# Attention beside key tiles: the other work in pieces of 128 tokens, and row sums inverted on VectorE

## The chip, the cores and the metric

The kernel runs on one core of a Trainium2 chip. The metric is the device time of one execution in microseconds; the median of three runs is shown, and one further execution was profiled. The engines are TensorE (PE in the profile, its weight loads PEld), VectorE (DVE), ScalarE (ACT), GpSimd (POOL) and SyncE (SP, which here only issues DMAs).

## What is computed

The input x has shape (4, 2048, 512). It is normalized over its last axis; the output is x plus attention plus a sparse expert layer, both of the normalized xn:

```python
qkv = xn @ w_qkv                     # 16 heads of 32
q, k = spectral_filter(q), spectral_filter(k)      # a fixed 32x32 map per head
attn = softmax(q @ k.T / sqrt(32)); a = (attn @ v) @ w_out + b_out
probs = softmax(xn @ w_gate)         # 8 experts, the best one, first 100 tokens of each
f = combine(dispatch(xn) @ w_expert + b_expert)
return x + a + f
```

All of it is in float32. The softmax needs a maximum and a sum of each row of 2048 scores; the row sums are inverted and multiplied onto the product with v before w_out.

## The kernel before

The spectral filter is folded into the weights at the start. Then the program goes through 16 head groups (k; 4 batches x 4 groups of 4 heads), in each through 4 query blocks of 512 tokens (n), and in each through 16 key tiles of 128 tokens (j). Two key tiles make a window (WIN, line 40). So there are 1024 tiles and 512 windows.

A tile's work (lines 918 to 938) is done for two pairs of heads, u = 0 and 1. TensorE writes minus the row maximum into two PSUM banks (`shift`, 3-row bf16 matmuls, negm in the profile), computes scores for a later block's maxima into two more (`max_matmuls`, k,q), and adds the scores (`scores`, q,k). ScalarE takes the exponential of each bank into an `even` or `odd` tile; VectorE reduces the maxima (`max_reduce`, part). Last come the products of the tile before with v (`products`), which VectorE adds to `num`. The eight banks are handed out in turn by `bank()`, whoever asks.

All other work is put behind the tiles as steps. The `agenda` holds a list for each window; a list's first half stands behind the even tile, the second behind the odd (lines 916, 917, 943). InOrder (line 71) keeps this order on every engine's queue, SP's included from line 786 on. What stands on the agenda:

- `projections(k + 1)`: twelve blocks of 512 tokens for the next group, 8 of `query_key` and 4 of `value`, placed at equal distances over the group. Each takes one bank and ends in one ScalarE copy. The weights wg have one buffer, so the load for group k + 2 follows the last block.
- `close_steps`, for each block that has ended: `fold` sums the exponentials over the partitions with TensorE and copies them (den). The four different rows travel to DRAM and back as a 128x16 tile (few), are inverted by VectorE, go to DRAM again and are spread over 32 partitions each (factor): seven DMAs on SP's queue. `divide` multiplies num by factor on GpSimd (ot). `result` projects 128 tokens with w_out (wo,ot) and copies them; `add` adds them to the output by an accumulating DMA.
- For a new batch: loading, `measure` (bn_stats on VectorE), `scale` (a power on GpSimd), `normalize` (ScalarE), `turn` (TensorE transposes of two token tiles, each copied by ScalarE), and the `route` of the expert layer, a chain of small steps and 16 scattering DMAs. The batch's groups 2 and 3 (k = 2, 3, 6, 7, 10, 11) carry this. From k = 12 on the expert layer itself is on the agenda.

At the start of each window stand the split of new maxima, an accumulating DMA (`pair`: even += odd of the window before) and GpSimd's running sums of the exponentials (`add_to`, two operations of 128x1024). With these GpSimd and the DMA engines have work in every window.

Of the kernel before, what the change touches and what calls it, by code (L numbers as in the profile page):

```python
# [38 lines left out]
SCALE = 1.0 / math.sqrt(DH)  # L39
WIN = 2  # L40
# [61 lines left out]
def attention_and_top1_experts(ctx: ExitStack, tc: tile.TileContext, a: dict, out: bass.AP):  # L102
# [118 lines left out]
    def token_stage(b):  # L221
# [38 lines left out]
        def turn(i):  # L260

            for j in (i, i + 1):
                px = bank()
                xn = held[j // TQ][:, j % TQ, :]
                for r in range(NR):
                    on.tensor.transpose(px[:, r * P : (r + 1) * P], xn[:, r * P : (r + 1) * P], ident)
                on.scalar.copy(xnT[:, :, j * P : (j + 1) * P], px.rearrange("p (r n) -> p r n", r=NR))
# [52 lines left out]
        def below_top():  # L320
            on.vector.reduce_max(top, logits, axis=AX.X)
            on.gpsimd.tensor_tensor(probs, logits, wide(top), ALU.subtract)
            on.scalar.activation(probs, probs, AF.Exp)
# [63 lines left out]
        route = [score, by_token, below_top, divide, best, ranked, first_best, place, carry_on, locate, note]  # L387
# [22 lines left out]
    def query_key(k, n, s):  # L410
        cols = slice(n * QB, (n + 1) * QB)
        pq = bank()
        for r in range(NR):
            columns(pq, wg[k][:, r, s, :], xnT[:, r, cols], start=(r == 0), stop=(r == NR - 1))
        if s == 0:
            qs[k, n] = qkv.tile([P, QB], F32, tag="q", name="q", bufs=5)
            on.scalar.copy(qs[k, n], pq)
        else:
            if n == 0:
                ks[k] = qkv.tile([P, S], F32, tag="k", name="k")  # L420
            on.scalar.copy(ks[k][:, cols], pq)

    def value(k, n):
        if n == 0:
            vs[k] = qkv.tile([P, NT, P], F32, tag="v", name="v")
        pv = bank()
        for t in range(TQ):
            i = n * TQ + t
            tok = slice(t * P, (t + 1) * P)
            for r in range(NR):  # L430
                columns(
                    pv[:, tok],
                    xnT[:, r, i * P : (i + 1) * P],
                    wg[k][:, r, 2, :],
                    start=(r == 0),
                    stop=(r == NR - 1),
                )
        on.scalar.copy(vs[k][:, n * TQ : (n + 1) * TQ, :], pv.rearrange("p (t d) -> p t d", t=TQ))

    def projections(k):  # L440

        order = [(query_key, 0, 1), (query_key, 0, 0)]
        order += [(query_key, n, 1) for n in range(1, NQ)] + [(query_key, 1, 0)]
        order += [(value, n) for n in range(NQ)] + [(query_key, n, 0) for n in range(2, NQ)]
        return [lambda f=f, at=at: f(k, *at) for f, *at in order]
# [203 lines left out]
    def close_steps(k, n, num, acc):  # L649
# [4 lines left out]
        def fold():  # L654
            den = work.tile([P, QB], F32, tag="den", name="den", bufs=1)
            on.scalar.copy(den, row_sums([acc]))
            held["sums"] = scratch.tile([HG, QB], F32, name="sums")
            on.sync.dma_start(out=held["sums"], in_=den[0::DH, :])

        def fold_here():  # L660

            held["factor"] = work.tile([P, QB], F32, tag="factor", name="factor", bufs=1)
            on.vector.reciprocal(held["factor"], row_sums([acc]))


        def fetch():
            held["few"] = small.tile([P, HG * QB // P], F32, name="few", bufs=2)
            on.sync.dma_start(out=held["few"], in_=held["sums"].rearrange("h (c e) -> (h c) e", e=HG * QB // P))

        def invert():  # L670
            on.vector.reciprocal(held["few"], held["few"])
            held["inverse"] = scratch.tile([HG, QB], F32, name="inverse")
            on.sync.dma_start(
                out=held["inverse"].rearrange("h (c e) -> (h c) e", e=HG * QB // P), in_=held["few"]
            )

        def spread():
            held["factor"] = work.tile([P, QB], F32, tag="factor", name="factor", bufs=1)
            for h in range(HG):
                on.sync.dma_start(  # L680
                    out=held["factor"][DH * h : DH * (h + 1)], in_=held["inverse"][h].partition_broadcast(DH)
                )

        def divide():
            held["ot"] = work.tile([P, QB], F32, tag="ot", name="ot", bufs=1)
            on.gpsimd.tensor_tensor(held["ot"], num, held["factor"], ALU.mult)
# [9 lines left out]
        if (k, n) == (B * NG - 1, NQ - 2):  # L696
            return [(3, fold_here), (4, divide), (5, result, 0), (5, result, 1), (6, result, 2), (6, result, 3), (7, add)]
        steps = [(2, fold), (3, fetch), (4, invert), (5, spread), (7, divide)]
        return steps + [(8, result, 0), (8, result, 1), (9, result, 2), (9, result, 3), (10, add)]
# [38 lines left out]
    first_projections = projections(0)  # L738
    scale(0, TQ, on.vector)
    for i in range(TQ):  # L740
        normalize(i)
        measure(TQ + i)
        if i % 2 == 1:
            turn(i - 1)
# [34 lines left out]
    ahead = {1: lambda: turn(4), 3: lambda: turn(6), 6: first_projections[2]}  # L779
    ahead.update({9: lambda: turn(8), 11: lambda: turn(10), 14: first_projections[3]})  # L780
    ahead.update({17: lambda: turn(12), 19: lambda: turn(14), 22: first_projections[4]})
    ahead.update({28: first_projections[5], 33: first_projections[6]})
    ahead.update({4 + j: lambda j=j: normalize(12 + j) for j in range(0, 2)})
    ahead.update({7 + j: lambda j=j: normalize(14 + j) for j in range(0, 2)})
    first_projections = first_projections[7:]
# [20 lines left out]
    GW = NQ * NW  # L806
    agenda = [[] for _ in range(B * NG * GW + 2 * NW)]

    def at(window, step, *args):
        agenda[window].append(lambda: step(*args))  # L810
# [11 lines left out]

    def place_experts(start):
# [3 lines left out]
        first = start + 18  # L827
        at(first, begin)
        for i in range(ST):
            at(first + 1 + i, fetch, i)  # L830
            at(first + 3 + i, measure, i)
        at(first + 11, scale)
        for i in range(ST + 2):
            at(first + 12 + i, expert, i)
        for i in range(ST):
            free = start + GW + i * NW + 11
            for step in (gather_row, add_row, scatter_row):
                at(free, step, i)
                free += 1

    def plan(k):

        b, c = divmod(k, NG)
        start = k * GW
        if k == 0:
            for i, step in enumerate(first_projections):
                at(i, step)
            for i, step in enumerate(first_route):
                at(NW + i, step)
            for n in range(NQ):  # L850
                at(1 + 4 * n, load, n)
                for i in range(TQ):
                    at(3 + 4 * n + i // 2, first_bias, n * TQ + i)
                at(5 + 4 * n, first_sums, n)
        if k == (B - 1) * NG:
            place_experts(start)
        if k + 1 == B * NG:
            return
        at(start + GW // 2, load_out_weights, k + 1)
        if k + 2 < B * NG:  # L860
            at(start + GW - 2, load_qkv_weights, k + 2)
        if k == 0:
            at(len(first_projections), load_qkv_weights, 1)
        first, last = len(first_projections) + 2 if k == 0 else 0, GW - 1
        if c == NG - 2 and b + 1 < B:

            at(start + 10, begin_stage, b + 1)
            for n, (come, go) in enumerate(((11, 19), (15, 23), (20, 28), (24, GW))):
                at(start + come, in_stage, 0, n)
                at(start + go, in_stage, 7, n)  # L870
            for i in range(NT):
                at(start + 13 + i + i // 8, in_stage, 1, i)
                at(start + 14 + i + i // 8, in_stage, 6, i)
            at(start + GW - 1, in_stage, 2)
            at(start + GW - 2, in_stage, 0, 0)
            at(start + GW + 1, in_stage, 0, 1)
        elif c == NG - 1:

            for n in (2, 3):
                at(start + 2 * n - 1, in_stage, 0, n)  # L880
            for i in range(NT):
                at(start + i // 2 + i // 8, in_stage, 3, i)
                if i % 2 == 1:
                    at(start + i // 2 + i // 8 + 1, in_stage, 4, i - 1)
            for i in range(len(first_route)):
                at(start + 10 + i, follow_route, i)
            first, last = 10, GW - 1
        steps = projections(k + 1)
        for i, step in enumerate(steps):
            at(start + first + (last - first) * i // len(steps), step)  # L890
# [12 lines left out]
    for k in range(B * NG):  # L903
        plan(k)
        for n in range(NQ):
            num = work.tile([P, QB], F32, tag="num", name="num")
            tiles = {}
            for w in range(NW):
                even, odd = w * WIN, w * WIN + 1
                if window in splits:  # L910
                    max_split(*splits.pop(window))
                if window in pairs:
# [3 lines left out]
                here = agenda[window]  # L916
                cut = (len(here) + 1) // 2
                for j in (even, odd):
# [24 lines left out]
                    for step in here[:cut] if j == even else here[cut:]:  # L943
# [12 lines left out]
            if not last:  # L956
                for after, *step in close_steps(k, n, num, tiles[NT - WIN]):
                    at(window + after, *step)
    products(*left)
    add_to(*adds.pop(window))  # L960
    for step in agenda[window]:
        step()
    close_last(k, n, num, [tiles[j] for j in (NT - 4, NT - 3, NT - 2, NT - 6, NT - 1)], y)
    for steps in agenda[window + 1 :]:
# [35 lines left out]
```

## Time and profile before

| | |
|---|---|
| median of 3 runs | 4454.81 us (4453.89 to 4457.47) |
| the profiled execution | 4463.09 us, its span 4461.3 us |
| mean granted TensorE clock | 0.993 |
| first key tile starts, last starts | 96.2 us, 4441.7 us |
| plain group 5 (1476.9 to 1738.5) | 261.6 us: PE 261.6, DVE 188.8, ACT 154.8, POOL 173.0 busy, DMA share 0.77 |
| group 2 (647.3 to 915.8) | 268.5 us: PE 266.3, DVE 200.3, POOL 190.3, DMA share 0.85 |
| group 3 (915.8 to 1212.1) | 296.3 us: PE 284.4, DVE 192.1, ACT 175.2, POOL 194.5, DMA share 0.73 |
| group 15 (4214.4 to 4441.7) | 227.3 us: PE 214.4, DVE 164.6, POOL 140.4, DMA share 0.87 |
| packets of the queue q1 (SP's DMAs) | 79,456, 93.89 MB, 7.0% of the DMA engines |

All instructions after the first few carry the line of one helper (L82), so they are told apart by their operands. A matmul in float32 leaves two records. The time of a matmul overlaps its neighbours', so the distance from one start to the next says more than the duration.

### The profile page before, as it was taken

What the parts mean: (1) busy time and instruction counts of PE and PEld (TensorE: products, weight loads), DVE (VectorE), ACT (ScalarE), POOL (GpSimd) and SP (SyncE); (2) the same over time, 40 slices, a digit from 0 to 9 for tenths busy, and PEclk for the clock granted to TensorE, in tenths of its full rate; (3) what the DMA queues carried; (4) which work ended last, traced back from release to release, by engine and by line L of the source; (5) the groups of instructions that cost most, each with busy time, mean ns of one, the idle gap of its engine ahead of it and who ended that gap; (6) DMA issues with size and microseconds to landing.
All of it is one profiled execution on the core that took longest, in us unless ns stands there. A gap on an engine that the chain in (4) does not pass through costs nothing. (4 is left out here: it accounts for less than half of the span.)

```text
span 4461.3 us, 106253 instructions
## 1 busy us (share of the span) xinstructions
PE 4369.7 (98%) x44398; PEld 1869.5 (42%) x44398; DVE 3130.6 (70%) x3634; ACT 2581.3 (58%) x4971; POOL 2958.8 (66%) x2009
## 2 busy tenths in 40 slices
PE   8999999999999999999999999999999999999998
PEld 4443443434434343443444434343443444434432
DVE  6667777766676777776667767777667676676776
ACT  3555565565555556556555555555655555555665
POOL 0677666775766766776677666767667674776773
PEclk9999999999999999999999999999999999999999
DMA  4677778886777777798677777888768876788788
GB/s 107 157 169 155 154 151 166 194 198 129 144 151 147 157 157 156 165 206 182 122 150 150 154 158 142 168 178 206 162 128 161 165 156 122 155 165 163 148 164 179
DMA packets 191546, 707.03 MB, mean 158 GB/s; under 512 B 47374, under 2 KB 52656, under 8 KB 125784
## 3 DMA queue, kind: packets, MB, share of 16 engines
q0 software_dynamic: 110432, 605.83, 69.6%
q1 hardware_dynamic: 79456, 93.89, 7.0%
q8 instruction: 347, 5.69, 0.5%
q14 instruction: 135, 1.11, 0.1%
q10 hardware_dynamic: 1176, 0.52, 0.0%
HBM read 76.03 MB, written 89.98 MB: 37 GB/s over the span
## 5 line engine op out<-in xcount | busy, mean ns | idle before, releaser
L82 DVE TENSOR_REDUCE part<-array 128x2 f32<-128x1024 f32 (+1 forms) x2313 | 2433.9, 1097 | 1218.5 <-PE array L82 1205.6
L82 POOL TENSOR_TENSOR even<-even 128x1024 f32<-128x1024 f32 x876 | 2133.1, 2550 | 215.1 <-DMA even<-odd 213.8
L82 PE MATMUL array<-k,q 32*128 32x512 f32 x8192 | 2221.7, 621 | 2.4 <-DVE part L82 1.7
L82 PE MATMUL array<-q,k 32*128 32x512 f32 x8192 | 2047.3, 593 | 1.3 <-issue 1.3
L82 ACT ACTIVATE even<-array 128x512 f32<-128x512 f32 x2048 | 1064.9, 601 | 453.0 <-PE array L82 443.1
L82 ACT ACTIVATE odd<-array 128x512 f32<-128x512 f32 x2048 | 1060.1, 602 | 434.7 <-issue 224.7
L82 POOL DMA_DIRECT2D even<-odd x510 | 460.1, 902 | 1101.7 <-ACT odd L82 887.8
L82 PEld LDWEIGHTS array<-k,q 32*128 32x128 f32 x8192 | 806.3, 183 | 167.7 <-DVE num L82 71.3
L82 PE MATMUL array<-negm,ones_b 3*128 3x512 bf16 x4096 | 792.4, 382 | 15.6 <-issue 5.2
L82 PEld LDWEIGHTS array<-q,k 32*128 32x128 f32 x8192 | 746.0, 185 | 13.2 <-issue 4.3
L82 DVE TENSOR_TENSOR num<-num,array 128x512 f32<-128x512 f32 x960 | 650.8, 678 | 34.4 <-PE array L82 19.3
L82 PEld LDWEIGHTS <-ones_b 3*128 3x128 bf16 x4096 | 202.1, 92 | 904.3 <-issue 776.6
L82 PE MATMUL array<-even,v 128*32 128x512 f32 x4096 | 548.8, 606 | 8.2 <-ACT odd L82 8.1
L82 PE MATMUL array<-odd,v 128*32 128x512 f32 x4096 | 548.4, 606 | 4.6 <-ACT even L82 4.5
L82 PE MATMUL array<-xnT,wg 128*32 128x512 f32 x4096 | 465.3, 595 | 1.8 <-DMA wg<-wd 1.1
L82 PE MATMUL array<-wo,ot 128*32 128x512 f32 x2048 | 264.4, 607 | 37.5 <-POOL ot L82 37.4
L82 PEld LDWEIGHTS array<-xnT,wg 128*32 128x32 f32 x4096 | 132.3, 110 | 307.9 <-issue 270.9
L82 PEld LDWEIGHTS array<-even,v 128*32 128x32 f32 x4096 | 81.0, 108 | 401.2 <-ACT odd L82 390.1
L82 ACT COPY y<-array 128x512 f32<-128x512 f32 x252 | 147.6, 586 | 173.8 <-PE array L82 173.0
L82 PEld LDWEIGHTS array<-odd,v 128*32 128x32 f32 x4096 | 81.1, 108 | 396.0 <-ACT even L82 388.0
L82 PEld LDWEIGHTS array<-wg,xnT 128*32 128x32 f32 x8192 | 227.0, 110 | 43.8 <-issue 26.2
L82 PE MATMUL array<-wg,xnT 128*32 128x128 f32 x8192 | 238.3, 273 | 2.7 <-issue 2.4
(127 smaller groups left out, 1370.6 us busy)
## 6 DMA issues: line engine op xcount, KB each, us to landing
even<-odd POOLq DMA_DIRECT2D x510, 1024.0 KB
out_dram<-y POOLq DMA_DIRECT2D x63, 1024.0 KB
xs<-in_L_attn_x_dram SPq DMA_DIRECT2D x30, 1024.0 KB
out_dram<-xs SPq DMA_DIRECT2D x16, 1024.0 KB
factor<-inverse SPq DMA_DIRECT2D x248, 64.0 KB
wg<-wd SPq DMA_DIRECT2D x15, 768.0 KB
wo<-in_L_attn_w_out_dram SPq DMA_DIRECT2D x16, 256.0 KB
negm<-row SPq DMA_DIRECT2D x192, 4.0 KB
```

The lines of the kernel that those rows point to most:

```text
L82: done = act(*args, **kwargs)
```

## The change

The agenda now has a list for each tile ("half") instead of each window, and a list of costs beside it. `query_key`, `value` and `turn` work on 128 tokens: a block becomes four pieces, each with its own bank and its own ScalarE copy; a query/key matmul has 128 columns and not 512. `spread` places a group's pieces in order, up to four tiles before the group's end, so that the sum of costs stays level; a piece, a result, a fold and a turn cost 1, a closing's inversion 0. The projections of the first group that run before the first tile remain whole.

`close_steps` copies the whole den, and eight `invert` steps of 64 columns, one behind each of eight tiles, invert it on VectorE; the seven DMAs and the scratch tensors are gone. `divide` moves from the agenda to `heads`, which stand at the start of a window, before pair and sums. Counted in tiles from the end of a block: fold 4 to 5, inversion 8 to 6-13, divide 14, results 16 to 19 become 15 to 18. For the last block but one of all: fold 7, two inversions behind each of tiles 8 to 11, divide 12, results 12 to 15. The route's exponential becomes a step of its own. The scale of a new batch moves from the last window of group 2 to four tiles before its end.

```diff
         def turn(i):
-            for j in (i, i + 1):
-                px = bank()
...
-                on.scalar.copy(xnT[:, :, j * P : (j + 1) * P], px.rearrange("p (r n) -> p r n", r=NR))
+            px = bank()
...
+            on.scalar.copy(xnT[:, :, i * P : (i + 1) * P], px.rearrange("p (r n) -> p r n", r=NR))
...
         def below_top():
             on.vector.reduce_max(top, logits, axis=AX.X)
             on.gpsimd.tensor_tensor(probs, logits, wide(top), ALU.subtract)
+
+        def exponentials():
             on.scalar.activation(probs, probs, AF.Exp)
...
-    def query_key(k, n, s):
-        cols = slice(n * QB, (n + 1) * QB)
-        pq = bank()
+    def query_key(k, n, s, first, last):
+        here, cols = slice(first * P, last * P), slice(n * QB + first * P, n * QB + last * P)
+        pq = bank()[:, here]
         for r in range(NR):
             columns(pq, wg[k][:, r, s, :], xnT[:, r, cols], start=(r == 0), stop=(r == NR - 1))
...
+            on.scalar.copy(qs[k, n][:, here], pq)
...
-    def projections(k):
+    def projections(k, tiles=1):
...
-        return [lambda f=f, at=at: f(k, *at) for f, *at in order]
+        return [
+            lambda f=f, at=at, t=t: f(k, *at, t, t + tiles) for f, *at in order for t in range(0, TQ, tiles)
+        ]
...
         def fold():
-            den = work.tile([P, QB], F32, tag="den", name="den", bufs=1)
-            on.scalar.copy(den, row_sums([acc]))
-            held["sums"] = scratch.tile([HG, QB], F32, name="sums")
-            on.sync.dma_start(out=held["sums"], in_=den[0::DH, :])
...
+            on.scalar.copy(held["den"], row_sums([ended[k, n][1]]))
...
-        def fetch():
...
-        def spread():
...
+        def invert(i):
+            at = slice(i * PART, (i + 1) * PART)
+            on.vector.reciprocal(held["factor"][:, at], held["den"][:, at])
...
-        steps = [(2, fold), (3, fetch), (4, invert), (5, spread), (7, divide)]
-        return steps + [(8, result, 0), (8, result, 1), (9, result, 2), (9, result, 3), (10, add)]
+            steps = [(7, 1, fold)] + [(8 + i // 2, 0, invert, i) for i in range(QB // PART)]
+            first = 12
+        else:
+            steps = [(5, 1, fold)] + [(6 + i, 0, invert, i) for i in range(QB // PART)]
+            first = 15
+        steps += [(first + t, 1, result, t) for t in range(TQ)]
+        return steps + [(first + TQ - 1 + first % 2, 0, add)], (first - first % 2, divide)
...
+    def spread(steps, last):
+        base = steps[0][1]
+        def places(level):
+            half, done, found = base, costs[base], []
+            for cost, first, _ in steps:
+                while half < first or done + cost / 2 > level * (half - base + 1):
+                    half += 1
+                    if half > last:
+                        return None
+                    done += costs[half]
+                done += cost
+                found.append(half)
+            return found
+        found = next(filter(None, (places(level / 32) for level in range(16, 400))))
...
-        steps = projections(k + 1)
-        for i, step in enumerate(steps):
-            at(start + first + (last - first) * i // len(steps), step)
+            done = spread([(1, ready if k == 0 else start, step) for step in pieces], last)
+        if k + 2 < B * NG:
+            at(done[-1] + 1, load_qkv_weights, k + 2)
...
                 if window in splits:
                     max_split(*splits.pop(window))
+                for step in heads[2 * window]:
+                    step()
                 if window in pairs:
                     pair(*pairs.pop(window))
...
-                    for step in here[:cut] if j == even else here[cut:]:
+                    for step in agenda[2 * window + (j == odd)]:
                         step()
```

## The prediction

> **What bounds the kernel now.** I read the page first, then the groups of instructions by form, TensorE's timeline tile by tile, the waits of TensorE, and last the busy times in stretches (one for each of the 16 head groups). From the page:
>
> ```profile
> span 4461.3 us, 106253 instructions
> PE 4369.7 (98%) x44398; PEld 1869.5 (42%) x44398; DVE 3130.6 (70%) x3634; ACT 2581.3 (58%) x4971; POOL 2958.8 (66%) x2009
> q8 instruction: 347, 5.69, 0.5%
> ```
>
> TensorE is the bound. What a key tile costs it is read from the timeline (start, duration, engine, operation, and in brackets the idle time before and its releaser), from the start of one tile's first shift matmul (negm) to the next tile's, and what a step behind a tile adds from the start of the products (even,v / odd,v) on:
>
> ```profile
> 1588.16 0.39 PE L82 MATMUL array<-negm,ones_b 3*128 3x512 bf16 x2
> ...
> 1590.30 1.07 PE L82 MATMUL array<-odd,v 128*32 128x512 f32 x8
> 1591.30 0.39 PE L82 MATMUL array<-negm,ones_b 3*128 3x512 bf16 x2
> ```
> ```profile
> 1580.59 1.06 PE L82 MATMUL array<-odd,v 128*32 128x512 f32 x8
> 1581.47 3.62 PE L82 MATMUL array<-xnT,wg 128*32 128x512 f32 x32
> 1585.02 0.39 PE L82 MATMUL array<-negm,ones_b 3*128 3x512 bf16 x2
> ```
> ```profile
> 1603.39 1.07 PE L82 MATMUL array<-odd,v 128*32 128x512 f32 x8
> 1604.28 3.68 PE L82 MATMUL array<-wg,xnT 128*32 128x128 f32 x128
> 1607.88 0.39 PE L82 MATMUL array<-negm,ones_b 3*128 3x512 bf16 x2
> ```
>
> A bare tile takes 3.14 us; products to next tile are 1.00 bare, 4.43 with a query/key block (+3.43), 4.49 with a value block (+3.49). One result adds 0.86, two 1.72: steps behind a tile add their pure time and no fixed cost. I compared all 1023 tile periods with 3.14 (2.20 at the end, where no maxima are left) plus such prices. What they take beyond that is 128 us in all; the rest is work. It is very uneven: groups 1, 5 and 9 have under 2 us each. So even placing has nothing to win in plain groups; it can only win back named stalls:
>
> ```profile
> PE array L82 <- POOL ot L82: 37.4, 15, 6.8
> PE array L82 <- issue: 9.9, 9, 2.8
> ```
> ```profile
> 807.21 0.39 PE L82 MATMUL array<-negm,ones_b 3*128 3x512 bf16 x2 [2.17 <-issue]
> 925.25 3.64 PE L82 MATMUL array<-wo,ot 128*32 128x512 f32 x16 [6.21 <-POOL ot L82]
> 1038.94 0.31 ACT L82 ACTIVATE probs<-probs 128x128 f32<-128x128 f32 x1 [3.38 <-POOL probs L82]
> 4253.19 0.25 DVE L82 RECIPROCAL few<-few 128x16 f32<-128x16 f32 x1 [1.52 <-DMA few<-sums]
> ```
> ```profile
> 801.00:811.00 10.00, 7.83 (x156) 5.28 (x148) 3.59 (x6) 2.42 (x5) 0.00 (x0) 0.83 0.94 159
> 915.00:930.00 15.00, 8.79 (x60) 2.66 (x56) 4.87 (x7) 4.33 (x9) 14.43 (x10) 0.79 0.82 221
> ```
>
> The stretches (length, busy time of PE, PEld, DVE, ACT and POOL, granted clock, DMA share, GB/s) show a second price: after an idle stop of about 1.8 us or more the granted clock is half for 3.4 us or twice that (mean 0.83 and 0.79 here), which costs 1.7 us or more on top. Excess of the tile periods by cause, throttle included:
> (1) Instruction supply, 22. Six stops of 1.1 to 2.8 us have no releaser that explains them (116, 805, 1373, 1941, 2210, 2988 us). Each lies in or just behind a value block and ends 2.2 to 2.5 us after a packet of the instruction queue starts; seven more value blocks are stretched by 0.5. A packet is 5.69 MB / 347 = 16.4 KB, and 88,796 matmuls and loads make 64 bytes each: 256 instructions, exactly what one value block issues in 3.5 us. A bare tile issues 56 in 3.14.
> (2) TensorE waits for GpSimd's ot at the start of groups 3, 7 and 11: 26.
> (3) The same wait elsewhere: 14, and 9 more in group 15.
> (4) ScalarE stands in order behind the route's exponential: 8.
> (5) VectorE stands in order behind a DMA round trip, in group 15: 4.5.
> (6) VectorE's bn_stats (0.69 + 0.18) behind a bare tile: 15 times 0.5, 8. VectorE's bare tile is 2.96 of 3.14, so it has no room.
> (7) Start, end, normalizations, experts, negm: about 36.
>
> **The change, part by part.**
> *Blocks cut to 128 tokens.* Value pieces cost what they cost now, a quarter of 3.49 = 0.87: that block already runs 128-column matmuls. Query/key blocks become the same shape: 122 blocks x (3.49 - 3.43) = **+7**. TensorE loads go from 1870 us busy to about 2300; loads of the value block (110 ns) already hide under matmuls of that shape. The Trainium skill, "TensorE: Matmul & The Clock Gate", section "Back-to-back issue gap", speaks against this cut: it gives about 81 ns a matmul at 128 columns and 131 at 512 in a sustained stream, so four quarters would cost 2.5 times a whole. An estimate from that page: each of 122 blocks goes from 3.43 to 8.5, +616 us. The two timeline rows above run both shapes, and their difference is 0.06; I go by them.
> ScalarE copies 740 pieces (0.29, the 128x128 copy's row) for 185 blocks (0.585): +106 us busy, price 0 on the path. A tile's exponentials end 3.4 us after its start, the piece at 4.0; its copy is done 0.45 into the next tile, which needs that bank again at 1.09 (second half's maxima). Without these 0.64 us of cover, each 0.1 would cost 74. Turns leave in 12 runs a batch, not 8; a run of transposes starts 0.17 later than back-to-back matmuls: 3 x 4 x 0.17 = **+2**.
> *Spread.* Nearly every tile of groups 0 to 14 gets a piece, a result or a fold: 4.0 us, against VectorE's 2.96 + 0.53. (6) mostly goes: **-6** of 8. (1): a block of 256 instructions now lasts 8.5 us (120 in 4.0), so a late packet has 5 us more to come; **-19** of 22, bounds 0 and -22. The Trainium skill, "Runtime: NRT & Kernel Launch", section "Instruction fetch mechanics", calls the cost of crossing a 16 KiB block mostly hidden; by that (1) would have another cause and these 19 would not come. The six packets that precede six stops decide for me.
> *Closing on VectorE.* 504 reciprocals of 128x64 replace 62 of 128x16, one of 128x512, and 434 DMAs on SP's queue. Rows: 128x16 0.246, 128x128 0.910; between them 64 columns are 0.246 + 48/112 x 0.664 = 0.53 (bounds 0.25 and 0.91): 267 us more on VectorE, 70 to 76%. Behind a covered tile 3.49 < 4.0: nothing; even at 0.91 it is 3.87. Behind a bare tile followed by a bare tile: 2.96 + 0.53 - 3.14 = 0.35. Group 15 has no pieces: 22 of them; the tiles 61 and 62 of each group, where the weights are reloaded, and group 13's start give about 22 more: 44 x 0.35 = **+15** (bounds 3 and 32). (5) goes: **-4.5**. SP no longer waits for sums and inverses ahead of negm and x loads; SP is not on the path, price 0, bounds 0 and -3.
> *Divide ahead of the window's pair and sums on GpSimd; results at tiles 15 to 18 instead of 16 to 19.* Pair issue and two sums (0.9 + 2 x 2.55, and the landing they wait for) no longer stand before ot; the deadline comes 4 us earlier. Against (3): **-19** of 23. What queues behind divide is the pair, which then starts 1.4 later; the sums are due a window (8 us) on. In groups 2, 6, 10 scale (3.8, mostly the power) moves three tiles up, out of ot's window: it ends some 14 us after tile 60 starts, against 13.4 when TensorE wants ot, and a late landing adds 1 to 4: (2) falls from 26 to 9, **-17** (bounds 0 and -26).
> *Exponentials as a step of its own:* ScalarE reaches it two tiles after GpSimd's subtraction, (4): **-8**. Weights for group 1 are asked for three tiles before use, no longer beside two 1 MB transfers; 1.3 now, 0 to 3 then, price 0. Two normalizations and a copy now meet behind some tiles of groups 3, 7, 11 (2.1 + 1.6 + 0.6 of ScalarE against 3.7): **+4** (bounds 0 and 12).
>
> Sum: -19 - 17 - 19 - 8 - 4.5 - 6 = -73.5; +7 + 2 + 15 + 4 = +28; net **-45.5**. The profiled execution took 4463.1 (span 4461.3), 8.3 above the median 4454.8; so 4417.6 for it and **4409** for the median.
>
> **The rivals.**
> *A, instruction supply gets worse (slower).* TensorE's instructions rise by 23,400 to 112,000 (+26%), 439 packets, and now every tile with a piece is dense. Some 6 of 63 value blocks were stopped, at 3 us; if one packet in ten of the 350 or so in such tiles were as late, that is 35 x 3 = 105: -45.5 + 105 = +59, 4514. It turns slower at (45.5 + 16) / 3, some 20 late packets. For: all stops were at the shape that the change spreads everywhere. Against: tiles of 56 instructions in 3.14 us never stopped, and 120 in 4.0 is nearer to that than 256 in 3.5.
> *B, ot stays late (hardly any change).* GpSimd's order changes little in groups 2 and 3, and landing of the accumulating DMAs decides. Then -36 of the sum stays away: -9.5, 4445. For: sums of group 2 wait up to 3.5 us for a landing just before the 6.2 us stop. Against: divide no longer stands behind those sums, and scale no longer in ot's window.
> *C, all goes.* (1) to (6) gone, 10 of (7) too, reciprocals half hidden: -92 - 10 + 20 = -82, 4373.
>
> **How the numbers follow.** Forecast (-25 to -65, 4390 to 4430): 0.48. C and between: 0.15. B (-25 to +9): 0.20, of it 0.10 faster, 0.09 the same. A or another slower course: 0.17. A measurement here tells 0.2% (9 us) from nothing. Faster 0.73, same 0.09, slower 0.18. The range reaches down to C and up past B into A's beginning, 4372 to 4468, leaving out most of A.
>
> **What would show it.** Right: a query/key piece's tile at 4.01 us; reciprocals near 530 ns; TensorE's wait for ot under 12 us in all; hardly any wait on issue; group 15 some 8 us longer less its ot waits; groups 3, 7, 11 each 8 to 14 us shorter; plain groups within 2 us. Wrong: tiles with a piece at 4.1 or more, new stops with no releaser, or VectorE's reciprocal ending TensorE's waits in groups that have pieces.

## The result and the profile after

The changed kernel takes **4420.24 us** (median of 4 runs, 4417.72 to 4421.32); the kernel before, run beside it, took 4454.35. The ratio is 0.9927, 95% interval 0.9909 to 0.9944: some 33 us or 0.7% faster. The forecast was 4409. The profiled execution took 4421.32 with a span of 4419.5, against 4463.09 before: 41.8 less, where the sum had 45.5. The size is near the forecast, but its parts are not.

The page of the changed kernel (spans, busy times, the queues q1 of SP's DMAs and q8 of instructions):

```profile
span 4419.5 us, 129899 instructions
...
PE 4331.3 (98%) x56110; PEld 2193.4 (50%) x56110; DVE 3340.1 (76%) x4059; ACT 2663.3 (60%) x5527; POOL 2942.4 (67%) x2009
...
q1 hardware_dynamic: 49200, 76.09, 5.4%
q8 instruction: 439, 7.19, 0.6%
```

VectorE has 209 us more to do and ScalarE 82; TensorE loses 38 us of busy time while it runs a quarter more instructions. A tile with a piece is as regular as forecast. In TensorE's timeline (start, duration, engine, operation) one tile runs from the first negm to the next:

```profile
803.53 0.39 PE L83 MATMUL array<-negm,ones_b 3*128 3x512 bf16 x2
...
806.55 1.06 PE L83 MATMUL array<-wg,xnT 128*32 128x128 f32 x32
807.54 0.39 PE L83 MATMUL array<-negm,ones_b 3*128 3x512 bf16 x2
```

That is 4.01 us: 3.14 for the bare tile and 0.87 for the piece. What TensorE waited for (in all, times, longest):

```profile
PE array L83 <- POOL ot L83: 42.9, 8, 11.1
PE array L83 <- ACT odd L83: 10.7, 20, 1.4
...
PE array L83 <- ACT even L83: 6.0, 9, 1.5
PE array L83 <- DVE num L83: 4.4, 2, 4.1
PE array L83 <- DVE part L83: 1.9, 4, 0.7
```

The line for issue (9.9 before) is gone, and the waits on ScalarE and VectorE are small. But the wait for ot, which was to fall under 12 us, has grown, with its longest now 11.1. Three stops of 11.1, 10.1 and 11.1 us at the end of groups 2, 6 and 10 make up 32 of the 42.9. In the stretches around the first of them (length, busy time of PE, PEld, DVE, ACT and POOL, granted clock, DMA share, GB/s) TensorE stands for most of 15 us and then runs on at a granted clock of 0.50 until 920.4, while GpSimd hardly rests:

```profile
900.00:905.00 5.00, 3.98 (x39) 1.43 (x36) 4.94 (x5) 2.55 (x6) 1.40 (x2) 1.00 1.05 286
905.00:920.00 15.00, 3.89 (x24) 1.08 (x20) 0.72 (x2) 1.80 (x4) 14.45 (x15) 0.56 0.34 100
```

GpSimd's timeline shows why (DMA_DIRECT2D is the issue of a transfer; the brackets give its idle time and what ended it):

```profile
863.51 1.28 POOL L83 DMA_DIRECT2D out_dram<-y  x1
864.29 1.41 POOL L83 DMA_DIRECT2D even<-odd  x1
...
866.07 1.74 POOL L83 DMA_DIRECT2D even<-odd  x1
879.71 4.67 POOL L83 TENSOR_TENSOR even<-even 128x1024 f32<-128x1024 f32 x2 [11.89 <-DMA even<-odd]
...
904.18 4.66 POOL L83 TENSOR_TENSOR even<-even 128x1024 f32<-128x1024 f32 x2 [3.60 <-DMA even<-odd]
908.81 1.25 POOL L83 TENSOR_TENSOR xs<-xs,b_out 128x512 f32<-128x512 f32 x1
...
910.50 2.94 POOL L83 TENSOR_TENSOR rstd<-rstd,power 128x16 f32<-128x16 f32 x1
...
915.67 1.25 POOL L83 TENSOR_TENSOR ot<-num,factor 128x512 f32<-128x512 f32 x1
```

At 863 to 867 an accumulating DMA of a result, two pairs and a store of xs (SP issued it at 867.0) leave almost together, 1 MB each. GpSimd waits 11.89 us for the pair's landing. From then on it has two sums, a bias and a pair for every window of some 8 us and gains little. So scale, which the agenda puts at tile 60 (started at 890.9), runs at 910, still right ahead of ot. ot starts at 915.67; TensorE wanted it at 905.9.

In the kernel before, GpSimd's order there was the same, scale (rstd) right ahead of ot, behind a shorter wait for the landing:

```profile
915.22 4.68 POOL L82 TENSOR_TENSOR even<-even 128x1024 f32<-128x1024 f32 x2 [3.50 <-DMA even<-odd]
...
920.35 2.94 POOL L82 TENSOR_TENSOR rstd<-rstd,power 128x16 f32<-128x16 f32 x1
...
923.94 1.26 POOL L82 TENSOR_TENSOR ot<-num,factor 128x512 f32<-128x512 f32 x1
```

The groups of GpSimd's sums and the new reciprocals (count | busy, mean ns | idle before):

```profile
L83 POOL TENSOR_TENSOR even<-even 128x1024 f32<-128x1024 f32 x876 | 2125.9, 2534 | 442.0 <-DMA even<-odd 434.6
L83 DVE RECIPROCAL factor<-den 128x64 f32<-128x64 f32 x504 | 273.9, 544 | 0.0
```

### The profile page after: what moved, and what is told of

It reads as the page before. It is cut to its first block, busy times and chain, and to the rows that moved or that the text cites. A ratio compares the mean times of both kernels' runs of the same rounds, so it can differ in the third digit from the quotient of the medians.

```text
span 4419.5 us, 129899 instructions
## 1 busy us (share of the span) xinstructions
PE 4331.3 (98%) x56110; PEld 2193.4 (50%) x56110; DVE 3340.1 (76%) x4059; ACT 2663.3 (60%) x5527; POOL 2942.4 (67%) x2009
## 4 chain that ended last, share of the span: by engine, by line
PE 88%; DMA 5%; POOL 4%; issue 2%; ACT 1%; DVE 1%; POOLq 0%; ACTq 0%; DVEq 0%
PE array L83 88%; DMA even<-odd 5%; POOL even L83 3%; POOL xs L83 0%; ACT odd L83 0%; POOL rstd L83 0%; DMA wg<-wd 0%; DVE part L83 0%; POOL ot L83 0%; ACT xg L83 0%; DMA odd<-in_L_attn_w_qkv_dram 0%; POOL rest L83 0%; DVE even L83 0%; ACT xs L83 0%; POOL row L83 0%
## 5 line engine op out<-in xcount | busy, mean ns | idle before, releaser
L83 PE MATMUL array<-k,q 32*128 32x512 f32 x8192 | 2156.8, 615 | 2.6 <-DVE part L83 1.9
L83 PEld LDWEIGHTS array<-q,k 32*128 32x128 f32 x8192 | 774.1, 186 | 80.6 <-issue 2.6
L83 PEld LDWEIGHTS array<-k,q 32*128 32x128 f32 x8192 | 731.8, 183 | 61.8 <-issue 15.0
L83 PEld LDWEIGHTS array<-xnT,wg 128*32 128x32 f32 x15808 | 450.7, 110 | 241.9 <-issue 135.3
L83 PE MATMUL array<-xnT,wg 128*32 128x128 f32 (+1 forms) x15808 | 529.4, 277 | 1.9 <-DMA wg<-wd 1.2
L83 PE MATMUL array<-wo,ot 128*32 128x512 f32 x2048 | 269.7, 600 | 43.0 <-POOL ot L83 42.9
L83 DVE RECIPROCAL factor<-den 128x64 f32<-128x64 f32 x504 | 273.9, 544 | 0.0
```

The source lines that it names most:

```text
L83: done = act(*args, **kwargs)
```

## The experiments

The kernels ran in four groups, each beside the kernel before, which took 4452 to 4457 there. So they are compared by the ratio to it; 0.001 is 4.5 us. The changed kernel stands at 0.9927 (0.9909 to 0.9944).

| run | median, us | ratio, 95% interval |
|---|---|---|
| scale behind ot | 4407.76 | 0.9904 (0.9888 to 0.9921) |
| results four tiles later | 4410.59 | 0.9910 (0.9894 to 0.9927) |
| scale behind ot, one result's DMA later | 4402.05 | 0.9875 (0.9860 to 0.9890) |
| value blocks whole | 4429.36 | 0.9938 (0.9922 to 0.9955) |
| query/key blocks whole | 4431.26 | 0.9942 (0.9925 to 0.9959) |
| all blocks whole | 4435.88 | 0.9963 (0.9950 to 0.9975) |
| all blocks whole, round trip | 4426.26 | 0.9929 (0.9914 to 0.9945) |
| round trip, one tile less | 4445.73 | 0.9972 (0.9959 to 0.9984) |
| no reciprocals | 4420.15 | 0.9922 (0.9909 to 0.9936) |
| scale behind ot, one result's DMA later, round trip | 4397.51 | 0.9873 (0.9856 to 0.9890) |
| ot on VectorE | 4643.26 | 1.0416 (1.0398 to 1.0433) |
| ot on VectorE, factor in the array | 4455.14 | 1.0007 (0.9998 to 1.0017) |

### Why ot is late at the end of groups 2, 6 and 10

**Scale behind ot.** The four small GpSimd instructions go behind the multiplication.

```diff
-            at(start + GH - 4, in_stage, 2)
+            heads[start + GH - 2].append(lambda: in_stage(2))
```

> The changed kernel, but in groups 2, 6 and 10 GpSimd's four scale instructions (3.97 us, 2.94 of it the power) stand behind ot's multiplication instead of ahead of it. Theory (GpSimd's order makes ot late at the end of these groups): each of the three stops of 10 to 11 us falls by 4, and with the half clock behind it by 4 to 5; 12 to 15 less in all, about 4407. Rival (the landing of the 1 MB pairs alone decides, and GpSimd would wait there anyhow): less than 3 gained, 4418 to 4421. A third outcome: normalize now waits for the scale, the turns at the start of groups 3, 7 and 11 come late, and what is won goes there (4419 to 4430, a wait of TensorE on ScalarE's copies of the turns).

It measured 0.9904: 10 us less than the changed kernel by the ratios (the intervals just overlap), 12.5 by the medians. The waits of TensorE, 42.9 in the changed kernel:

```profile
PE array L83 <- POOL ot L83: 29.5, 8, 7.0
```

The three stops fell from 10 to 11 us to 6.5 to 7.0 each, by about the scale's 3.97. The turns of the next group did not wait. So GpSimd's order is a third of the stop, and 7 us stay.

**Results four tiles later.**

```diff
-            first = 15
+            first = 19
...
-        return steps + [(first + TQ - 1 + first % 2, 0, add)], (first - first % 2, divide)
+        return steps + [(first + TQ - 1 + first % 2, 0, add)], (14 if first > 12 else 12, divide)
```

> The changed kernel, but the four results of a query block are asked for four tiles later (tiles 19 to 22 of the next block instead of 15 to 18); ot's own place in GpSimd's order stays. Theory (the three stops and the small ones are a deadline that GpSimd misses by at most 11 us, and nothing more): four tiles are 12.6 to 16 us, so TensorE waits for ot nowhere for long; 42 of the excess at tiles 191, 447 and 703 and some 5 more go, and a few come back where results now meet the normalizations at the start of a group: 4373 to 4385. Rival (DMA engines and GpSimd have too much to do there, so a later deadline moves the stop to the sums of the next window, which VectorE's last maxima wait for): 4405 to 4425, with a wait on even or num in its place.

It measured 0.9910, 8 us less by the ratios (with overlapping intervals) and not the 35 to 47 of the theory, which so falls. The waits of TensorE:

```profile
PE array L83 <- DMA negm<-row: 40.5, 7, 10.7
...
PE array L83 <- POOL ot L83: 3.2, 2, 1.7
```

The wait for ot is nearly gone, and one of the same length has come in its place: negm, the row maxima of the next block. GpSimd splits them into row and rest just ahead of ot, and SP's DMA carries them on. In this run's timelines GpSimd ends the split at 911.5 and TensorE goes on:

```profile
913.27 0.61 PE L83 MATMUL array<-negm,ones_b 3*128 3x512 bf16 x2 [9.78 <-DMA negm<-row]
```

So not one step's deadline is short: GpSimd's whole queue is about 10 us behind there, and whatever of it TensorE needs first is named. The rival was right in kind, though it looked for the wait at the sums. This edit moved more than the deadline, though: the accumulating DMA stands behind the results and also went four tiles later. GpSimd's wait of 11.89 is 4.42 in this run, with 7.92 two sums later, and ot starts at 911.48, 4.2 us sooner.

**One accumulating DMA four tiles later**, on top of scale behind ot.

```diff
-        return steps + [(first + TQ - 1 + first % 2, 0, add)], (first - first % 2, divide)
+        later = 4 if k % NG == NG - 2 and n == 1 else 0
+        return steps + [(first + TQ - 1 + first % 2 + later, 0, add)], (first - first % 2, divide)
```

> As the run with the scale behind ot (4408), and in groups 2, 6, 10 and 14 the accumulating DMA of the second block's result is issued four tiles later, so that its 1 MB no longer leaves within 3.5 us of two pairs and the store of xs. Theory (that meeting of 4 MB costs GpSimd the 12.2 us wait for the pair's landing, which it never makes up before the end of the group): the wait falls to 5 to 8 us, ot and the maxima's split come 4 to 6 us sooner, and the three stops of 7 to 8 shrink to 1 to 4 each: 4388 to 4398. Rival (DMA engines have too much in the whole stretch; the same wait appears a window later): 4403 to 4411, a wait of 10 us or more on even<-odd behind the later add.

It measured 0.9875, 13 us below the run with the scale behind ot by the ratios (the medians, from two groups of runs, differ by 6), between the ranges of its theory and its rival. GpSimd's timeline with the scale behind ot alone:

```profile
878.78 4.68 POOL L83 TENSOR_TENSOR even<-even 128x1024 f32<-128x1024 f32 x2 [12.20 <-DMA even<-odd]
...
910.09 1.25 POOL L83 TENSOR_TENSOR ot<-num,factor 128x512 f32<-128x512 f32 x1
```

and in this run:

```profile
869.78 4.68 POOL L83 TENSOR_TENSOR even<-even 128x1024 f32<-128x1024 f32 x2 [4.44 <-DMA even<-odd]
...
892.51 4.67 POOL L83 TENSOR_TENSOR even<-even 128x1024 f32<-128x1024 f32 x2 [7.92 <-DMA even<-odd]
906.35 1.25 POOL L83 TENSOR_TENSOR ot<-num,factor 128x512 f32<-128x512 f32 x1
```

The 12.20 us that this wait took with the scale behind ot alone became 4.44, as the theory had it; but 7.92 came back two sums later, behind the moved DMA, as its rival had it. ot starts at 906.35 instead of 910.09, and the three stops are 4.8 to 5.6, together 4.9 us less. Both theories hold in part. That the four 1 MB transfers meet is a cause of the 12.20, shown by taking one away; most of that time comes back where the DMA now leaves, and 3.7 us of it are gone when ot starts. The stretch as a whole is also full: from 880 to 905 us the DMA share is 0.99 in this run and 0.93 in the changed kernel.

### Dense blocks and the instruction supply

**Value blocks whole**, then **query/key blocks whole**: the rest as changed, a whole block counted as 4 for the spreading.

```diff
+    WHOLE = value          # in the other run: query_key
...
-            lambda f=f, at=at, t=t: f(k, *at, t, t + tiles) for f, *at in order for t in range(0, TQ, tiles)
+            w = TQ if f is WHOLE else tiles
+            made += [(lambda f=f, at=at, t=t, w=w: f(k, *at, t, t + w), w) for t in range(0, TQ, w)]
```

> The changed kernel (4420 us), but value blocks whole again (512 tokens, cost 4 for the spread); query/key stays in pieces. Theory 1, instruction supply at value blocks: TensorE's stops without a releaser come back at or just behind value blocks, some 5 to 7 of them and a few stretched blocks, 15 to 25 us with half-clock stretches: 4435 to 4445. Theory 2, the gain came from the level load on GpSimd and the DMA engines: 63 blocks out of 185 are lumps again, no stops without releaser; GpSimd's ot comes late at more places: 4425 to 4435, with TensorE's waits on ot above 43 us. If neither holds: 4418 to 4422.

> The changed kernel, but query/key blocks whole again (512 tokens in one bank, 512-column matmuls, cost 4); value stays in pieces. Theory 1: a whole query/key block issues 64 instructions in 3.43 us, so no stop without a releaser comes back, and the 7 us that the 128-column shape costs is saved: 4410 to 4416. Theory 2, level load is what counts: 122 lumps of 3.43 us bring back late ot and late landings: 4425 to 4440.

They measured 0.9938 and 0.9942. Both intervals overlap that of the changed kernel, so neither loss (5 and 7 us by the ratios) is settled by itself. Neither has a stop on issue: TensorE's waits on it are 0.5 and 0.2 us in all, although the first has value blocks of 256 instructions again. That the query/key blocks would gain 4 to 10 by being whole did not come. The times lie in the ranges of the second theories, but what these gave as the reason did not come: TensorE's wait for ot is 40.5 and 38.9 us, not more than 42.9.

**All blocks whole** from group 1 on, and **all blocks whole with the row sums closed by the round trip**, with the four tiles from fold to reciprocal that the kernel before had.

```diff
-        pieces = projections(k + 1)
+        pieces = projections(k + 1, TQ)
...
-            done = spread([(1, ready if k == 0 else start, step) for step in pieces], last)
+            done = spread([(TQ, ready if k == 0 else start, step) for step in pieces], last)
```

> The changed kernel with all blocks of groups 1 to 15 whole, spread by their cost of four units; closing, heads and turns as changed. Theory 1 of the prediction (a dense value block outruns the instruction packets): stops without a releaser return, four to eight of them, 1 to 3 us each, with the half clock 12 to 22; bn_stats and reciprocals behind bare tiles 10 to 15 more; cheaper query/key blocks 7 less: 4436 to 4450. Theory 2 (those stops had another cause in the kernel before, which left with the round trip through memory or with the order of the steps): no stop on issue, only what the value and the query/key blocks showed one by one, 9 + 11: 4436 to 4444. The two are told apart by the stops, not by the time.

> Blocks whole as in the run of 4436, and the row sums closed as in the kernel before, by a round trip through memory with its four tiles between fold and reciprocal. Theory (the six stops of the kernel before need both: a dense block, and the round trip's 30,256 small packets that delay the packets of the instruction queue): stops without a releaser are back, waits of TensorE on issue come to 6 to 12 us, and the time to 4450 to 4465. Rival (neither made them; they belonged to the places that the spreading gave up): waits on issue under 2 us, and 4436 plus what the round trip alone costs, 0 to 15: 4436 to 4451.

The first measured 0.9963, 16 us above the changed kernel, with the intervals apart; its TensorE waits on issue:

```profile
PE array L83 <- issue: 0.5, 1, 0.5
```

and in the second run, at 0.9929:

```profile
PE array L83 <- issue: 2.0, 5, 0.9
```

The kernel before had 9.9 us, nine times, up to 2.8. Whole value blocks of 256 instructions are there in both runs, packets of the instruction queue start inside 46 and 45 of the 60 tiles that have one (32 of 63 before, counted from the packet records; inside the block itself 35, 37 and 12), and a packet takes 1.0 us in all of these kernels. Still the stops stay away, with the round trip's small packets too. Nor is it the packet's place in the block: before, all 11 blocks in which one started 1.8 to 3.7 us after the block's first matmul lost 0.27 us or more, up to 2.2; in the first of these runs 15 such blocks lost at most 0.19. So a dense block with a packet in it is not enough to stop TensorE; what in the places of the kernel before made the six is open.

The two runs say something else. With whole blocks, the closing on VectorE costs more than the round trip: 0.9963 against 0.9929, 15 us by the ratios, 10 by the medians. That it is the reciprocals is argued from the tiles; no run with whole blocks leaves them out. There most tiles are bare; one with a bn_stats and a reciprocal (tile 58 of group 2) is 0.92 longer than its price, against 0.51 with bn_stats alone, and the rest is spread thinly over many tiles. And whole blocks with the round trip, at 4426 below both ranges of the expectation, end level with the changed kernel: cutting the blocks and moving the inversion together brought nothing that can be measured over the rest of the change.

### The closing on VectorE

**The round trip back**, first with one tile less between fold and fetch than before (fold at 5, fetch 6, reciprocal 8, spreading 10):

```diff
-            steps = [(5, 1, fold)] + [(6 + i, 0, invert, i) for i in range(QB // PART)]
+            steps = [(5, 1, fold_out), (6, 0, fetch), (8, 0, invert_few), (10, 0, spread_out)]
```

> The changed kernel, but the row sums of all blocks up to the last but one go through DRAM again (four DMAs out and back and spread, one reciprocal of 128x16 instead of eight of 128x64), at tiles 5, 6, 8 and 10 behind the block's end; everything else as changed. Theory 1: the eight reciprocals cost TensorE almost nothing where a piece stands (3.26 + 0.87 is above VectorE's work) and 0.12 us behind bare tiles, so 2 to 4 us are saved and the VectorE wait on the round trip, 4.5 us in group 15, comes back: 4418 to 4424. Theory 2, my own term of the prediction: 15 us of the changed kernel are reciprocals behind bare tiles: 4405 to 4412.

It measured 0.9972, 20 us above the changed kernel and above both ranges. VectorE stands in order behind the landing of few, and TensorE behind VectorE:

```profile
PE array L83 <- DVE part L83: 21.3, 10, 3.9
```

```profile
DVE few L83 <- DMA few<-sums: 36.7, 13, 6.0
```

The kernel before lost 4.7 us there, three times. This undid more than the change did, so it says what a short distance costs, not what the round trip costs.

**No reciprocals:** GpSimd multiplies by a tile of ones, so the result is not divided by the row sums.

```diff
-            held["factor"] = work.tile([P, QB], F32, tag="factor", name="factor", bufs=1)
+            held["factor"] = unit
...
-            on.vector.reciprocal(held["factor"][:, at], held["den"][:, at])
+            pass
```

> The changed kernel without its 504 reciprocals: GpSimd multiplies by a tile of ones, so that the result is not divided by the row sums. VectorE is 274 us less busy. Theory of the prediction (44 reciprocals stand uncovered at 0.35 each): 15 less, and GpSimd's wait of 86 us in all for the factor gone, which ends nothing on the path: 4403 to 4409. Rival (the profile after: tiles with a reciprocal and no piece are 0.12 longer): 5 less, 4413 to 4419. If GpSimd's wait for the factor is what makes it late in groups 2, 6 and 10, the three stops fall as well: below 4400.

It measured 0.9922, the same as with them (2 us less by the ratios, intervals some 6 wide to each side), and the three stops stayed at 10.6 to 11.1. 274 us of VectorE's work cost at most a few us; 15 is outside, the rival's 5 within.

**The 4402 version** (scale behind ot, one accumulating DMA later) **with the round trip** at its old distance:

```diff
-            steps = [(5, 1, fold)] + [(6 + i, 0, invert, i) for i in range(QB // PART)]
+            steps = [(5, 1, fold_out), (7, 0, fetch), (9, 0, invert_few), (11, 0, spread_out)]
```

> The version that took 4402 (scale behind ot, one result's accumulating DMA later), with one difference: the row sums of the 62 blocks go by the round trip through memory again, with the four tiles between fold and reciprocal that the kernel before had. Theory (closing on VectorE was worth nothing by itself: without its reciprocals the changed kernel took the same, and with whole blocks the round trip at four tiles shows no wait of VectorE on it): within 6 of 4402, 4396 to 4408. Rival 1 (the 25 lost with the round trip at three tiles belong to the round trip): 4415 to 4427, and TensorE's waits on VectorE's part come to 15 us or more. Rival 2 (the 10 that the round trip gained between the two kernels with whole blocks are VectorE's relief): 4388 to 4396.

It measured 0.9873 against 0.9875, median 4397.51: the same. VectorE's wait for few is down from 36.7 to

```profile
DVE few L83 <- DMA few<-sums: 11.3, 5, 4.4
```

So beside cut blocks either closing will do, if the round trip gets its distance. This and the 4402 version are faster than both kernels.

### ot on VectorE

The other way to make ot punctual is to take it off GpSimd.

```diff
-            on.gpsimd.tensor_tensor(held["ot"], ended[k, n][0], held["factor"], ALU.mult)
+            on.vector.tensor_tensor(held["ot"], ended[k, n][0], held["factor"], ALU.mult)
```

> The changed kernel, but ot = num x factor on VectorE (0.69 us, 128x512) at the same places, so that TensorE's results no longer depend on GpSimd's queue. Theory 1, what is left is ot's place in GpSimd's order: the stops of 11.1, 10.1 and 11.1 us at the ends of groups 2, 6 and 10 and the 9 us in group 15 vanish with their half-clock stretches, 45 to 55 us: 4368 to 4378. Theory 2, GpSimd and the DMA engines are simply over-full in groups 2, 6 and 10, and the stop only lets them catch up: then the running sums are late instead, TensorE or ScalarE waits for even tiles or for fold, and only 5 to 20 us come: 4400 to 4415.

It measured 1.0416, 4643 us, far above both ranges; TensorE waits 158.5 us behind VectorE's maxima (part). The groups on VectorE, where num's addition has one operand in the array (PSUM) and ot's has both in SBUF:

```profile
L83 DVE TENSOR_TENSOR num<-num,array 128x512 f32<-128x512 f32 x960 | 651.0, 678 | 47.3 <-PE array L83 36.4 <-ACT odd L83 6.4 <-ACT even L83 2.6
L83 DVE TENSOR_TENSOR ot<-num,factor 128x512 f32<-128x512 f32 x63 | 253.8, 4029 | 1.9
```

The same shape takes 0.68 us and 4.03. Sorted by what GpSimd did meanwhile, the 12 that ran beside none of its sums took 0.68 us (median), the 45 that met two of them 5.30, at most 7.82. Two sums are 4.67, and 4.67 + 0.68 = 5.35: VectorE seems to stand until GpSimd has ended both, with no turn between them. The Trainium skill, "SBUF — State Buffer", section "SBUF: two separate sides", says that a VectorE instruction with two SBUF inputs and a GpSimd instruction that reads SBUF exclude each other. The run after tests it: ScalarE first copies the factor into a bank.

```diff
+            copy = bank()
+            on.scalar.copy(copy, held["factor"])
-            on.gpsimd.tensor_tensor(held["ot"], ended[k, n][0], held["factor"], ALU.mult)
+            on.vector.tensor_tensor(held["ot"], ended[k, n][0], copy, ALU.mult)
```

> ot on VectorE as in the run that took 4643, but ScalarE first copies the factor into a bank of the array (about 0.6 us), so that VectorE multiplies an SBUF operand by one from the array. Theory (two SBUF operands collide with GpSimd's sums; with one of them in the array they do not): ot takes 0.65 to 0.75 us instead of 4.0, waits for ot go, VectorE and ScalarE each have 40 us more in covered tiles: 4378 to 4400. Rival (VectorE's full row of work at that place is what was stretched, whatever the operands): ot still takes 2 us or more and the time is above 4480.

```profile
L83 DVE TENSOR_TENSOR ot<-num,array 128x512 f32<-128x512 f32 x63 | 43.3, 687 | 51.5 <-ACT array L83 51.5
```

0.69 us, as the theory had it, for the 50 that met one of GpSimd's sums as for the other 13: the operand's place was the cause, and the page's sentence holds here. The time did not follow, 1.0007, no gain over the kernel before. VectorE now stands 51.5 us behind the copy, TensorE waits 16.2 us for ot on VectorE, 26 times, and 15.0 for negm, the backlog again. The expectation of 4378 to 4400 missed that VectorE, in order, reaches ot before ScalarE has done the copy. An earlier copy was not tried.

## Why the prediction was right, and where it was not

All 1023 tile periods were compared with the tile prices once more. Their excess is 74 us, against 128 before. (With each kind of tile priced at its shortest it is 93 against 145; the difference, 52 to 54, hardly depends on the prices.) The row with (6) and (7) is what the other rows leave.

| step | forecast | by the two profiles |
|---|---|---|
| (1) instruction supply | -19 | -22 |
| (2) ot at the end of groups 2, 6, 10 | -17 | +16 |
| (3) ot elsewhere | -19 | -11 |
| (4) exponential, (5) round trip | -12.5 | -12.5 |
| (6), (7), reciprocals, normalizations | +13 | -24 |
| query/key pieces, turns | +9 | +12 |
| sum | -45.5 | -41.5 |

- **Tile prices** were right: 4.01 us with a piece of either kind; the +616 us of the estimate that the prediction set against the cut did not come. The 64-column reciprocal took 0.544, forecast 0.53.
- **(1)** went in size, but not for the reason given. Packets may have had a part in the six stops, but a packet in a dense block is not enough, as the runs with whole blocks show. Rival A rested on that same mechanism; it did not come.
- **(2) is the step that failed.** The text put scale "no longer in ot's window", from the agenda's places, and a late landing at 1 to 4 us. The landing cost 11.89, GpSimd reached scale 19 us after its tile in the agenda had begun, and so scale still stood ahead of ot. Beside this the results were asked for one tile earlier. Measured from the start of the next group's first tile (905.4 without the stop), ot came 11.6 us later, against 9.4 before, and it was wanted 2.8 sooner: together the 4.9 by which the first stop grew (6.21 to 11.11). Rival B had the right mechanism, but (2) alone cost more than it allowed for, as (3) went. The sign that groups 3, 7 and 11 would be 8 to 14 us shorter came nearly (16.0, 15.0 and 12.2 by the starts of their first tiles), but not for its reason: groups 2, 6 and 10 are 7.0, 6.3 and 9.8 longer, as the stop now falls ahead of the group's end.
- **(3)** went, except in group 15: 7.9 us of excess at one tile (a stop of 4.84 and what follows it) some 80 us before the end, which no run here was aimed at.
- **Reciprocals +15** were mis-sized. Bare tiles with one in group 15 take 3.26 in a row, so 0.12 longer and not 0.35: the sum added durations, while back to back VectorE's instructions start before the one ahead has ended (0.60 from num's start to the reciprocal's, where num's duration is 0.68); 44 x 0.12 = 5, and the run without them gives 2 with 6 to either side.
- **(7) was left as it was**, and this hid the largest gain that the sum lacked. Before, tiles with bn_stats, two results, a copy of experts or a normalization behind them each took 0.45 to 0.7 more, some forty of them; spreading gives each only one such thing. Some 15 us more lie in 59 tiles with the transposes of the maxima (square, neg): those with nothing else took 3.59 (median) and take 3.34 now. With all blocks whole most of them take 3.34 too, so it is not the pieces; which other part of the change it is, is open. What a level load is worth by itself no run shows: all blocks whole were 16 us slower with the closing on VectorE, and level with the round trip.
- **The half clock** that the prediction puts behind stops of about 1.8 us or more is no rule: before, it followed 10 of the 13 such stops between 100 us and the last tile; after three, of 2.2 to 2.7 us (ended at 2132, 3219 and 3956), the granted clock stayed at 1.00.

So two errors of some 35 us each, of opposite sign, left the sum 4 us off by the two profiles. That they cancel is luck; by the medians, the forecast of 4409 is 11 us too low.

## What to carry to other kernels

When an engine runs behind, the agenda's places say nothing about who stands ahead of whom in time; read from the trace how far behind it is at that place, and find the wait in which it fell behind. Moving the deadline of the work that TensorE waits for here mostly brought up the next thing from the same queue; take work or a colliding transfer out ahead of it instead. Spreading small work one piece to a tile makes cover that can hide work that would cost elsewhere: the closing on VectorE cost 10 to 15 us more than the round trip among whole blocks, and nothing that can be measured among pieces.

## What the runs showed of the hardware that was not expected

A VectorE multiplication of two SBUF tiles of 128x512 took 0.68 us alone and 5.30 (median, up to 7.82) beside two GpSimd sums; with one operand in the array it took 0.69, beside a sum too. Matmuls of 128 columns for query/key cost 0.873 us a piece against 0.858 for a quarter of the 512-column block. Six stops that each ended 2.2 to 2.5 us after the start of an instruction packet did not return with the same dense blocks, packets of the same length and the same small transfers, in another order. In the changed kernel the granted clock was 0.50 for 13.7 us around the first long stop; in the kernel before it was 0.50 for 3.4 or 6.8 us at a time, behind most stops of 1.8 us or more but not behind all.
